# A four-layer kernel: layer 0's chain by quarters, layer 1's norm in two parts, layer 2's end together with layer 3's start

## The chip, the cores and the metric

The kernel runs on one core of one Trainium2 chip. TensorE (PE) multiplies matrices, VectorE (DVE) and ScalarE (ACT) do elementwise work, GpSimd (POOL) does some of it and issues gathers, SyncE (SP) issues most DMAs. Every engine works through its own queue in order, and semaphores let one wait for another. The metric is the device time of one execution in microseconds (us).

## The reference, cut to what matters

The input x has 8 sequences of 512 tokens with 128 channels. Four layers follow, each of the form

```python
xn = _layernorm(x)
x = x + attn(xn) * _silu(ffn(xn))
```

Layer 0's attn is a recurrence over the 512 tokens, for each sequence and each of 16 heads with an 8x8 state S. What follows the recurrence matters here:

```python
sab = einsum('bhvk,bhk->bhv', S, kk_)
S = S * exp(w_)[:, :, None, :] + sab[..., None] * b_[:, :, None, :] + v_[..., None] * k_[:, :, None, :]
y = einsum('bhvk,bhk->bhv', S, r_)
...
yn = (y - y.mean(-1)) / sqrt(var + 0.00064) * ln_w + ln_b
bonus = (r4 * k4 * time_faaaa).sum(-1) * v4
out = (yn + bonus) * g @ output.T
```

Its ffn has 48 experts that each choose tokens. Layer 1 is linear attention with Taylor features and 8 experts that choose 1024 tokens each. Layer 2 is causal attention whose result is refined by 8 iterations `u = tanh(ctx @ w_ctx + xs @ w_x + b)`, `vs += 0.1 * (u - xs - vs)`, `xs += 0.1 * vs`; its ffn is a chain of ternary products. Layer 3 is a Mamba-like mixer, and its ffn is full attention over 512 tokens with 16 heads.

## The kernel before

x lies in SBUF as 32 tiles of 128 tokens (4 per sequence, JT = 4). The program runs layer after layer.

**Layer 0** works in four blocks (jt) of 128 tokens of all sequences; 128 partitions are sequence times head. A block is 64 pair-steps (HT), in 8 chunks of SH = 8. For each pair-step DVE does five pairs of small operations (L747 to L759) on the state, for each chunk also Z (L734, L738) and HR (L761 to L765), the state times r. `outputs` (L691) sums HR over 8 with PE and copies the sum to Y by ACT: `eighths` (L360) is 8 products with the identity, each in two passes, which accumulate in PSUM (L364). Between the chunks `go_on` takes steps of the next block's projections (`front`, L386 to L487, and `back`, L643 to L680: PE turns Kt, Rt, KNt, EWt, Bt, Vt, ACT copies, L663 and its neighbours combine pairs of tokens), and `side` takes steps of the 48 experts. When a block's last chunk is done, the chain L772 to L814 follows for the whole block: own value (L772, L773), mean by eighths (L777), square (L778), variance by eighths, Ln and Exp (L779, L780), bonus (L781), Y times mu (L782), eight scalings by ACT (L784), 32 passes to turn it (L796), gate (L799), and the product with `output` (L804 to L810). For block 3 it ends in x (L813, L814).

In layers 0 to 2 PE's order is the program's (manual_schedule); the other engines' order is made by the framework's scheduler, which moves an instruction ahead where its operands are ready by its own cost model. Pools reserve SBUF; a pool that takes over memory waits for its last users.

**Layer 1** begins with `layernorm`: the 32 tiles in two groups of 16, for each group 16 statistics (L143), seven small operations of 128x16 (L147 to L154), 16 normalisations, 10 of them on DVE (L158) and 6 on ACT (L160). Then 32 transposes (L168) and the first product for k (L1082).

**Layer 2** goes through 128 units of attention; `groups` and `rest` (the output product, the 8 iterations L1557 to L1565, the ternary chain L1580 to L1593 and the sum into x, L1603) are taken in steps beside the units of the next sequence. For the last sequence the steps remain and are run to the end (`layer2`, last two lines).

**Layer 3** then loads its constants and works in an order written out by hand on PE, DVE, ACT and POOL. A unit is one of 128 (sequence, group of heads, key tile): scores (L2089), maxima (L2091), exponentials (L2094), weighing (L2119). `begin` (L1812 on) makes a sequence's features and then its mixer parameters, `mixer` works for one of 32 tiles, `end` finishes a sequence; `fill` takes their steps between the units, with SHARE = 1.75 passes of credit, mixers from unit 9 on every third unit. Steps of `begin` that are still left when a mixer needs them are run in one go. After the units come the last mixers and ends.

Of the kernel before, what the change touches and what calls it, by code (L numbers as in the profile page):

```python
# [20 lines left out]
P = 128  # L21
# [59 lines left out]
class Kern:  # L81
# [53 lines left out]
    def layernorm(self, pool, x, xn, eps, nt=NT, group=16):  # L135

        nc = self.nc
        st = pool.tile([P, nt, 6], F32, name="ln_st")
        var, r, mr = (pool.tile([P, nt], F32, name="ln_" + n) for n in ("var", "r", "mr"))
        for g in range(0, nt, group):  # L140
            sl = slice(g, g + group)
            for j in range(g, g + group):
                nc.vector.bn_stats(st[:, j, :], x[:, j, :])  # L143

            mean = lambda i: st[:, sl, 3 * i + 1]
            dev = lambda i: st[:, sl, 3 * i + 2]
            nc.vector.tensor_tensor(r[:, sl], mean(0), mean(1), ALU.subtract)  # L147
            nc.vector.tensor_tensor(r[:, sl], r[:, sl], r[:, sl], ALU.mult)
            nc.vector.tensor_tensor(var[:, sl], dev(0), dev(1), ALU.add)
            nc.vector.scalar_tensor_tensor(var[:, sl], r[:, sl], C / 4.0, var[:, sl], ALU.mult, ALU.add)  # L150
            nc.vector.tensor_tensor(mr[:, sl], mean(0), mean(1), ALU.add)
            nc.scalar.activation(r[:, sl], var[:, sl], AF.Sqrt, bias=eps, scale=1.0 / C)
            nc.vector.reciprocal(r[:, sl], r[:, sl])
            nc.vector.scalar_tensor_tensor(mr[:, sl], mr[:, sl], -0.5, r[:, sl], ALU.mult, ALU.mult)  # L154
            for j in range(g, g + group):
# [175 lines left out]
def layer0(k, x, A, at):  # L331
# [5 lines left out]
    with ExitStack() as ctx:  # L337
# [212 lines left out]
        w1p_ = pool("l0w", 2)  # L550
        ep = pool("l0e", 2)
# [141 lines left out]
        for jt in range(JT):  # L693
# [79 lines left out]
            nc.vector.tensor_tensor(yp[:, :, 0, :], yp[:, :, 0, :], t3[:, 0:HT], ALU.add)  # L773


            mu = bp.tile([P, P], F32, name="mu")
            nc.vector.scalar_tensor_tensor(Y, Y, 8.0, bc(eighths(Y), 2, 8), ALU.mult, ALU.subtract)  # L777
            nc.scalar.activation(t3, Y, AF.Square)  # L778
            nc.scalar.activation(mu, eighths(t3), AF.Ln, bias=k.eps_gn, scale=1.0 / 8)  # L779
            nc.scalar.activation(mu, mu, AF.Exp, scale=-0.5)  # L780
            nc.vector.tensor_tensor(t3, Vs.rearrange("p t s n -> p (t s) n"), bc(bonus, 2, 8), ALU.mult)  # L781
            nc.vector.tensor_tensor(Y, Y, bc(mu, 2, 8), ALU.mult)  # L782
            for n in range(8):
                nc.scalar.activation(  # L784
                    Y[:, :, n], Y[:, :, n], AF.Identity, scale=cn["ln_w"][:, n : n + 1], bias=cn["ln_b"][:, n : n + 1]
                )

# [4 lines left out]
            for n0 in range(0, 8, 4):  # L792
                ps = k.pa((P, 4, P))
                for i in range(4):
                    for src in (Y, t3):
                        nc.tensor.matmul(  # L796
                            ps[:, i, :], src[:, :, n0 + i], k.ident, start=(src is Y), stop=(src is t3)
# [170 lines left out]
class Layer1:  # L968
# [6 lines left out]
    def __init__(self, k, cp, x, A, at):  # L975
# [3 lines left out]
        self.f_d = k.f1_d  # L979
        self.cn = k.load_consts(cp, A["c1"], at, "c1")  # L980
        self.xT = cp.tile([P, N], F32, name="xT1")
# [332 lines left out]
class Layer2(BySequence):  # L1314


    def __init__(self, k, ctx, x, A, at):
        self.k, self.x = k, x
        nc, tc = k.nc, k.tc
        pool = lambda name, bufs=1: ctx.enter_context(tc.tile_pool(name="l2" + name, bufs=bufs, reuse_waits="tile"))  # L1320
        cp = pool("c")
        self.cn = cn = k.load_consts(cp, A["c2"], at[0], "c2")
        self.fn = fn = k.load_consts(cp, A["f2"], at[1], "f2")

        self.half_s = cp.tile([P, 4], F32, name="half_s")
        nc.vector.tensor_scalar(self.half_s, fn["w1_s"], 0.5, None, ALU.mult)
        self.both_s = cp.tile([P, 4], F32, name="both_s")
# [9 lines left out]
        self.va2 = [cp.tile([P, JT, H * 9 + 23], F32, name=f"va2{i}") for i in range(2)]  # L1337
# [4 lines left out]
        self.mpad = [cp.tile([P, JT, P], F32, name=f"mpad{i}") for i in range(2)]  # L1342
        for t in self.mpad:
            nc.gpsimd.memset(t, 0.0)
        self.sp2 = pool("p", 2)
        self.tp = pool("t", 2)
# [7 lines left out]
    def begin(self, b):  # L1354
# [14 lines left out]
        h = tp.tile([P, JT, C], F32, name="h2", bufs=1)  # L1369
        nc.vector.tensor_tensor(h, xn, bc(r, 2, C), ALU.mult)  # L1370
        yield 0.0
        q["xT"] = tp.tile([P, T], F32, name="xT2", bufs=1)
# [4 lines left out]
        xa = tp.tile([P, T], F32, name="xa2", bufs=1)  # L1377
# [4 lines left out]
        q["qT"] = tp.tile([P, 4, T], F32, name="qT2")  # L1382
        q["kT"] = tp.tile([P, 2, T], F32, name="kT2")
# [224 lines left out]

# [709 lines left out]
```

## Time and profile before

| | us |
|---|---|
| median of three runs | 3602.8 (3601.02 to 3603.73) |
| profiled execution | 3603.68 |
| its span | 3602.0 |
| DVE busy | 2322.8 (64%) |
| PE busy | 2864.4 (80%) |
| ACT busy | 1790.3 (50%) |
| POOL busy | 729.9 (20%) |
| mean granted TensorE clock | 0.862 |
| layer 0's last HR starts | 838.22 |
| layer 1's first k product starts | 891.46 |
| layer 2's last x is added | 2611.36 |
| layer 3's first maxima start | 2626.50 |

Times are from the span's start. The profile's busy time of PE counts matmuls; weight loads (PEld) run beside them. A stretch row gives, for each engine, busy time and number of instructions, then the granted clock (1.00 is full) and the DMA engines' share. A timeline row gives start, duration, engine, line and operation, and in brackets how long the engine had been idle and what ended that. A row of waits gives the total, the number of times and the longest.

### The profile page before, as it was taken

The numbers are of one execution on the slowest core, as the hardware profiler recorded it, in microseconds if no ns is written. First come the engines' busy times: TensorE is split into PE (matmuls) and PEld (weight loads), VectorE is DVE, ScalarE is ACT, GpSimd is POOL, SyncE is SP. The second block draws the span as 40 slices with busy tenths as digits, with TensorE's granted clock in tenths as the row PEclk, the third lists the DMA queues.
The fourth block names the chain that finished last, engine by engine and source line by source line (L and its number), as shares of the span: only waits on it lengthen the run. The fifth ranks groups of instructions, "written<-read, shape, count | busy, mean of one in ns | idle before, by whom it ended". The sixth has DMA issues, their size and how long they took to land.

```text
span 3602.0 us, 46273 instructions
## 1 busy us (share of the span) xinstructions
PE 2864.4 (80%) x16950; PEld 1575.1 (44%) x16950; DVE 2322.8 (64%) x6354; ACT 1790.3 (50%) x3382; POOL 729.9 (20%) x845
## 2 busy tenths in 40 slices
PE   6175868635988898798888898898588798888887
PEld 4154656534444454333334333443235454444443
DVE  7999888896582334435455454554368777777775
ACT  4173646412544455254454554455255565666665
POOL 0012131300225553101111111111112221212221
PEclk8587889766899999899999999999678888888888
DMA  4012121211001222000000000000000000000000
GB/s 121 2 30 44 31 52 32 43 49 34 1 13 37 39 42 47 37 1 1 1 1 1 1 1 1 1 1 1 2 20 1 4 4 3 2 4 4 4 1 7
DMA packets 67523, 64.59 MB, mean 18 GB/s; under 512 B 5344, under 2 KB 59616, under 8 KB 66784
## 3 DMA queue, kind: packets, MB, share of 16 engines
q1 hardware_dynamic: 39264, 42.75, 3.9%
q0 software_dynamic: 19712, 14.69, 3.1%
q10 hardware_dynamic: 8320, 4.19, 0.4%
q8 instruction: 133, 2.18, 0.3%
q14 instruction: 94, 0.77, 0.1%
HBM read 43.80 MB, written 17.83 MB: 17 GB/s over the span
## 4 chain that ended last, share of the span: by engine, by line
PE 34%; DVE 14%; ACT 10%; issue 2%; POOL 1%; DMA 0%; POOLq 0%; ACTq 0%; DVEq 0%; SPq 0%
PE pu L1454 6%; PE ph L1435 5%; PE pu L2089 5%; DVE nm L2091 2%; PE pf L2119 2%; ACT at L2094 2%; PE pf L1503 2%; ACT at L1490 2%; ACT L1490 1%; PE pa L1557 1%; DVE mpad L1469 1%; PE pu L1466 1%; PE pa L1580 1%; PE pa L2132 1%; PE pa L2027 1%
## 5 line engine op out<-in xcount | busy, mean ns | idle before, releaser
L2094 ACT ACTIVATE at<-pu,nm 128x512 f32<-128x512 f32 x512 | 348.0, 691 | 195.9 <-DVE nm L2091 193.4
L2091 DVE TENSOR_REDUCE nm<-pu 128x1 f32<-128x512 f32 x512 | 319.0, 682 | 90.7 <-PE pu L2089 90.6
L2089 PE MATMUL pu<-qT,kT 32*128 32x512 f32 x1024 | 285.8, 732 | 87.6 <-ACT at L2094 87.2
L199 POOL TENSOR_SCALAR_AFFINE_SELECT at<-at 128x512 f32<-128x512 f32 x184 | 125.1, 680 | 1024.4 <-ACT at L1490 878.0
L1469 DVE TENSOR_REDUCE mpad<-pu 128x2 f32<-128x1024 f32 (+3 forms) x256 | 199.0, 819 | 148.8 <-PE pu L1466 148.7
L1128 ACT ACTIVATE at<-pu,rsqrt 128x1024 f32<-128x1024 f32 (+3 forms) x256 | 191.1, 793 | 188.0 <-PE pu L1123 160.7
L1435 PE MATMUL ph<-hid,f 128*128 128x512 f32 x512 | 255.5, 626 | 11.6 <-ACT hid L1436 11.5
L1490 ACT ACTIVATE at<-pu 128x1024 f32<-128x1024 f32 (+3 forms) x256 | 167.0, 701 | 163.7 <-PE pu L1454 162.7
L364 PE MATMUL pa<-HR,ident 128*128 128x128 f32 x512 | 127.8, 418 | 140.2 <-DVE HR L765 140.2
L364 PEld LDWEIGHTS pa<-HR,ident 128*128 128x128 f32 x512 | 112.7, 265 | 150.2 <-DVE HR L765 74.6
L2089 PEld LDWEIGHTS pu<-qT,kT 32*128 32x128 f32 x1024 | 95.3, 212 | 177.9 <-ACT at L2094 162.5
L2119 PE MATMUL pf<-at,va 128*32 128x512 f32 x1024 | 165.0, 723 | 1.9 <-POOL va L2106 1.9
L608 POOL DMA_INDIRECT f_d<-ys,idx x48 | 87.8, 1828 | 384.6 <-ACT ys L607 355.1
L1454 PE MATMUL pu<-kT,qT 32*128 32x512 f32 (+3 forms) x1024 | 134.9, 500 | 30.0 <-ACT at L1490 29.2
L1454 PE MATMUL pu<-qT,kT 32*128 32x512 f32 (+3 forms) x1024 | 128.0, 492 | 20.7 <-DVE mpad L1469 20.2
L1435 PEld LDWEIGHTS ph<-hid,f 128*128 128x128 f32 x512 | 94.1, 198 | 113.2 <-issue 89.2
L2106 POOL TENSOR_TENSOR va<-V,sm 128x32 f32<-128x32 f32 x128 | 33.7, 263 | 489.0 <-DVE sm L2105 488.4
L1123 PE MATMUL pu<-qT,kT 32*128 32x512 f32 (+3 forms) x1024 | 128.4, 507 | 5.3 <-ACT at L1128 4.4
L1066 POOL DMA_INDIRECT f_d<-ys,idx x64 | 102.8, 1606 | 142.7 <-DMA f_d<-ys,idx 86.0
L1490 ACT ACT_TABLE_LOAD x66 | 84.7, 1283 | 87.8 <-PE pu L1454 87.0
L1133 DVE TENSOR_TENSOR at<-at,ceiling 128x512 f32<-128x512 f32 x72 | 49.9, 695 | 105.6 <-ACT at L1128 99.9
L691 ACT COPY Y<-pa 128x128 f32<-128x128 f32 x32 | 8.5, 265 | 208.7 <-PE pa L364 208.7
(621 smaller groups left out, 6772.5 us busy)
## 6 DMA issues: line engine op xcount, KB each, us to landing
w<-in_w_dram SPq DMA_DIRECT2D x24, 512.0 KB
f_d<-zeros ACTq DMA_DIRECT2D x8, 512.0 KB
xn_d<-xn SPq DMA_DIRECT2D x8, 512.0 KB
w<-in_w_dram SPq DMA_DIRECT2D x16, 256.0 KB
w<-in_w_dram SPq DMA_DIRECT2D x24, 128.0 KB
f<-in_f_dram SPq DMA_DIRECT2D x1, 2888.0 KB
xn<-in_x_dram SPq DMA_DIRECT2D x4, 512.0 KB
Gt<-in_x_dram SPq DMA_DIRECT2D x4, 512.0 KB
```

What stands on the lines that cost most here:

```text
L199: self.nc.gpsimd.affine_select(a, a if src is None else src, pattern, ALU.is_ge, 0.0, base=0, channel_multiplier=-1)
L364: nc.tensor.matmul(ps, k.ident, src[:, :, i], start=(i == 0), stop=(i == 7))
L1123: nc.tensor.matmul(pu[:, n, 0:m], q["kT"][r, g // 2, kc * P : kc * P + P], q["qT"][r, g, kc * P :], start=True, stop=True,)
L1128: nc.scalar.activation(at_[:, i : i + 2, 0:m], pu[:, :, 0:m], AF.Square, bias=k.rsqrt2, scale=32.0**-0.5)
L1435: nc.tensor.matmul(ps, fn[n][:, c0 : c0 + P], src[:, i, :], start=(i == 0), stop=(i == 3))
L1454: self.k.nc.tensor.matmul(pu[:, n, 0:m], a[r, c0 : c0 + P], b[r, q0 : q0 + m], start=True, stop=stop)
L1469: nc.vector.tensor_reduce(top[:, i : i + 2, 16 + g % 2], pu[:, :, 0:m], AX.X, ALU.max)
L1490: nc.scalar.activation(at_[:, i : i + 2, 0:m], pu[:, :, 0:m], AF.Exp, scale=8.0**-0.5)
L2089: nc.tensor.matmul(pu, q["kT"][r, kc * P : (kc + 1) * P], q["qT"][r, g, :], start=True, stop=True)
L2091: nc.vector.tensor_reduce(nm[:, n : n + 1], pu, AX.X, ALU.max, negate=True)
L2094: nc.scalar.activation(E[:, n, :], pu, AF.Exp, bias=nm[:, w], accum_out=sm[:, w])
L2119: nc.tensor.matmul(po[i * 32 : i * 32 + 32, :], va[:, kc, c0 : c0 + 32], E[:, i, :], start=(kc == 0), stop=(kc == JT - 1))
```

## The change

First, `layernorm` takes parts. Layer 1's norm is done for the three tiles of each sequence that blocks 0 to 2 have finished (24 tiles) and then for the last ones (8 tiles). Its pools, and those of layer 0's experts, lie at the right end of the memory, apart from layer 0's other pools. In the changed order of DVE 24 statistics, the small operations and six normalisations stand between block 3's chunks, ten normalisations after the last HR; the transposes stay together behind the last tiles.

Second, `settle` does layer 0's chain up to Y times mu for a quarter of a block (two chunks), in three steps that the loop takes one per chunk, in all four blocks; a quarter's sums are products of 32 columns. The fourth quarter and the third's last step follow the last chunk. The bonus is now kept in Vs. L721, L724 and L732 of the changed kernel are the lines L773, L777 and L782 of before; L825 is L799.

Third, layer 2 hands what is left of its last sequence to layer 3 as `k.tail`. Layer 2's pools are split into a left part, which is released before layer 3, and a right part, which is released when the tail is done; layer 3's pools that need that memory are made by `more_pools` then. Layer 3 takes a step of the tail after each step of `begin(0)` and then one or two per unit. `begin` no longer runs on into the parameters, which are a list of their own, the attention's end (`attended`) is split off `end`, and SHARE, EARLY and EVERY change. Layer 2's constants c2 go to the right, too, and are loaded early in layer 1.

```diff
-    def layernorm(self, pool, x, xn, eps, nt=NT, group=16):
+    def layernorm(self, pool, x, xn, eps, parts=None):
         nc = self.nc
-        st = pool.tile([P, nt, 6], F32, name="ln_st")
-        var, r, mr = (pool.tile([P, nt], F32, name="ln_" + n) for n in ("var", "r", "mr"))
-        for g in range(0, nt, group):
-            sl = slice(g, g + group)
-            for j in range(g, g + group):
+        st = pool.tile([P, NT, 6], F32, name="ln_st")
+        var, r, mr = (pool.tile([P, NT], F32, name="ln_" + n) for n in ("var", "r", "mr"))
+        for part in parts or (slice(0, NT // 2), slice(NT // 2, NT)):
+            if parts:
+                tiles = [b * JT + j for b in range(B) for j in range(JT)[part]]
+                pick = lambda a: a.rearrange("p (b j) -> p b j", j=JT)[:, :, part]
+            else:
+                tiles, pick = range(NT)[part], lambda a: a[:, part]
+            for j in tiles:
                 nc.vector.bn_stats(st[:, j, :], x[:, j, :])
+            mean = lambda i: pick(st[:, :, 3 * i + 1])
+            dev = lambda i: pick(st[:, :, 3 * i + 2])
+            pv, pr, pm = pick(var), pick(r), pick(mr)
...
-        w1p_ = pool("l0w", 2)
-        ep = pool("l0e", 2)
+        w1p_ = pool("l0w", 2, side="right")
+        ep = pool("l0e", 2, side="right")
...
+            mu = bp.tile([P, P], F32, name="mu")
+            def settle(c, Y=Y, yp=yp, mu=mu, Vs=Vs, bonus=bonus, kr=kr):
+                pr, tk = slice(c * 16, c * 16 + 16), slice(c * 32, c * 32 + 32)
+                own_v = bp.tile([P, 16, 8], F32, name="own_v")
+                nc.vector.tensor_tensor(own_v, Vs[:, pr, 0, :], bc(kr[:, pr], 2, 8), ALU.mult)
+                nc.vector.tensor_tensor(yp[:, pr, 0, :], yp[:, pr, 0, :], own_v, ALU.add)
+                yield
+                y = Y[:, tk, :]
+                nc.vector.scalar_tensor_tensor(y, y, 8.0, bc(eighths(y), 2, 8), ALU.mult, ALU.subtract)
+                square = bp.tile([P, 32, 8], F32, name="square")
+                nc.scalar.activation(square, y, AF.Square)
+                v = Vs.rearrange("p t s n -> p (t s) n")[:, tk, :]
+                nc.vector.tensor_tensor(v, v, bc(bonus[:, tk], 2, 8), ALU.mult)
+                yield
+                nc.scalar.activation(mu[:, tk], eighths(square), AF.Ln, bias=k.eps_gn, scale=1.0 / 8)
+                nc.scalar.activation(mu[:, tk], mu[:, tk], AF.Exp, scale=-0.5)
+                nc.vector.tensor_tensor(y, y, bc(mu[:, tk], 2, 8), ALU.mult)
+                yield
+            settling = []
             last = None
             for o in range(0, HT, SH):
                 if jt == JT - 1 and o // SH >= HT // SH - JT:
                         nc.vector.tensor_tensor(s_v[:, :, j, :], f, old, ALU.add)
                     else:
                         held = f, old
+                for works in settling:
+                    next(works, None)
                 next(side, None)
                 go_on(3)
                 if last:
                     outputs(*last)
+                    if o // SH % 2 == 0:
+                        settling.append(settle(o // SH // 2 - 1))
+                        next(settling[-1])
...
             outputs(*last)
+            settling.append(settle(3))
             go_on(40)
             ready = made
-            t3 = fp.tile([P, B, C], F32, name="EWt").rearrange("p b (h n) -> p (b h) n", n=8)
-            nc.vector.tensor_tensor(t3[:, 0:HT], Vs[:, :, 0, :], bc(kr, 2, 8), ALU.mult)
-            nc.vector.tensor_tensor(yp[:, :, 0, :], yp[:, :, 0, :], t3[:, 0:HT], ALU.add)
-            mu = bp.tile([P, P], F32, name="mu")
-            nc.vector.scalar_tensor_tensor(Y, Y, 8.0, bc(eighths(Y), 2, 8), ALU.mult, ALU.subtract)
-            nc.scalar.activation(t3, Y, AF.Square)
-            nc.scalar.activation(mu, eighths(t3), AF.Ln, bias=k.eps_gn, scale=1.0 / 8)
-            nc.scalar.activation(mu, mu, AF.Exp, scale=-0.5)
-            nc.vector.tensor_tensor(t3, Vs.rearrange("p t s n -> p (t s) n"), bc(bonus, 2, 8), ALU.mult)
-            nc.vector.tensor_tensor(Y, Y, bc(mu, 2, 8), ALU.mult)
+            for step in chain(*settling):
+                pass
             for n in range(8):
                 nc.scalar.activation(
                     Y[:, :, n], Y[:, :, n], AF.Identity, scale=cn["ln_w"][:, n : n + 1], bias=cn["ln_b"][:, n : n + 1]
                 )
+            added = Vs.rearrange("p t s n -> p (t s) n")
...
-        with tc.tile_pool(name="l1a", bufs=2, reuse_waits="tile") as tp, tc.tile_pool(name="l1a1", bufs=1, reuse_waits="tile") as tp1:
+        right = lambda name, bufs: tc.tile_pool(name=name, bufs=bufs, reuse_waits="tile", side="right")
+        with right("l1a", 1) as tp, right("l1a1", 1) as tp1:
             xn = tp1.tile([P, NT, C], F32, name="xn1")
-            k.layernorm(tp, x, xn, k.eps5)
+            k.layernorm(tp, x, xn, k.eps5, parts=(slice(0, JT - 1), slice(JT - 1, JT)))
...
-        for _ in chain(groups, rest):
-            next(front, None)
+        assert next(front, None) is None
+        k.tail = chain(groups, rest), late.close
...
-        SHARE = 1.75
-        EARLY, EVERY = 9, 3
-        at = lambda b, jt: max(b * U + jt * JT - 2, EARLY + EVERY * (b * JT + jt))
-        mixers, begins, ends = [], [L.begin(0)], []
-        while not L.q or "ready" not in L.q[0]:
-            next(begins[0])
+        SHARE = 1.9
+        EARLY, EVERY = 19, 10 / 3
+        at = lambda b, jt: max(b * U + jt * JT - 2, EARLY + int(EVERY * (b * JT + jt)))
+        mixers, begins, parameters, ends = [], [], [], []
+        tail, release = k.tail
+        for _ in L.begin(0):
+            next(tail, None)
         credit = 0.0
         def fill():
             nonlocal credit
             credit = min(credit, SHARE) + SHARE
-            for works in (mixers, ends, begins):
-                for w in works[:1] if works is begins else list(works):
+            for works in (mixers, begins, parameters, ends):
+                for w in list(works) if works is mixers else works[:1]:
                     if works is mixers or credit > 0.0:
                         cost = next(w, None)
                         if cost is None:
                         else:
                             credit -= cost
+        def whole(works):
+            for w in works:
+                for _ in w:
+                    pass
+            works.clear()
         for n in range(B * U + LAG + 1):
             for b in range(B):
                 for jt in range(JT):
                     if n == at(b, jt):
-                        for w in begins if "cos" not in L.q[b] else ():
-                            for _ in w:
-                                pass
-                            begins.remove(w)
-                            break
+                        if "cos" not in L.q[b]:
+                            whole(parameters)
                         mixers.append(L.mixer(b, jt))
-                if b and n == max((b - 1) * U, at(b - 2, JT - 1) + 4 if b > 1 else 0):
+                if b and n == max((b - 1) * U, 1):
                     begins.append(L.begin(b))
-                if n == max((b + 1) * U + LAG, at(b, JT - 1) + 1):
-                    ends.append(L.end(b))
-                    next(ends[-1])
+                if b and n == b * U - 1:
+                    whole(begins)
+                if b and n == max((b - 1) * U + 8, at(b - 1, JT - 1) + 1 - U, at(b - 2, JT - 1) + 1 if b > 1 else 0):
+                    while "V" not in L.q.get(b, ()):
+                        next(begins[0])
+                    parameters.append(L.parameters(b))
             scores = L.scores(*divmod(n, U)) if n < B * U else iter(())
             next(scores, None)
+            if tail and next(tail, False) is False:
+                tail = None
+                release()
+                L.more_pools()
+                parameters.append(L.parameters(0))
             fill()
             next(scores, None)
             if LAG <= n < B * U + LAG:
-                L.weigh(*divmod(n - LAG, U))
+                b, u = divmod(n - LAG, U)
+                L.weigh(b, u)
+                if u == U - 1:
+                    assert not tail
+                    L.attended(b)
+                    ends.append(L.end(b))
             if 1 <= n <= B * U:
                 L.scale(*divmod(n - 1, U))
+            if tail and n % 2:
+                next(tail, None)
             fill()
         while mixers or ends:
             fill()
```

More of the change, by code (lines that the diff above doesn't have):

```diff
@@ L794, in layer0 @@
                 for i in range(4):
-                    for src in (Y, t3):
+                    for src in (Y, added):
                         nc.tensor.matmul(
-                            ps[:, i, :], src[:, :, n0 + i], k.ident, start=(src is Y), stop=(src is t3)
+                            ps[:, i, :], src[:, :, n0 + i], k.ident, start=(src is Y), stop=(src is added)
                         )
@@ L1335, in __init__ @@
         nc.vector.tensor_scalar(self.g1[:, 1:2], cn["b1"], 100.0, None, ALU.mult)
-        self.va2 = [cp.tile([P, JT, H * 9 + 23], F32, name=f"va2{i}") for i in range(2)]
+        self.va2 = [ap.tile([P, JT, H * 9 + 23], F32, name=f"va2{i}") for i in range(2)]
         for t in self.va2:
@@ L1340, in __init__ @@
             nc.gpsimd.memset(self.by_head(t)[:, :, :, 8:9], 1.0)
-        self.mpad = [cp.tile([P, JT, P], F32, name=f"mpad{i}") for i in range(2)]
+        self.mpad = [ap.tile([P, JT, P], F32, name=f"mpad{i}") for i in range(2)]
         for t in self.mpad:
             nc.gpsimd.memset(t, 0.0)
-        self.sp2 = pool("p", 2)
-        self.tp = pool("t", 2)
+        self.sp2 = right("p", 2)
+        self.tp = right("t", 2)
+        self.bp = pool("b", 2)
         self.ep = pool("e", LAG + 2)
@@ L1607, in layer2 @@
 def layer2(k, x, A, at):
+    late = ExitStack()
     with ExitStack() as ctx:
         ctx.enter_context(k.banks("l2p", pu=2, pf=1, pa=2, ph=1))
-        L = Layer2(k, ctx, x, A, at)
+        L = Layer2(k, ctx, late, x, A, at)
         units = [(b, g, kc) for b in range(B) for g in range(4) for kc in range(JT)]
@@ L1857, in begin, with parameters @@
         q["held"], q["po"] = {}, {}
-        q["ready"] = True
         yield 0.0
-        yield from self.parameters(q)
-    def parameters(self, q):
+    def parameters(self, b):
         k, nc, cn, tp, ap = self.k, self.k.nc, self.cn, self.tp, self.ap
+        q = self.q[b]
         xT = q["xT"]
@@ L2136, in end @@
         nc.scalar.copy(z, ps)
+    def end(self, b):
+        k, nc, fn, tp, q = self.k, self.k.nc, self.fn, self.tp, self.q[b]
+        z = q["z"]
         sq = self.squares(z, JT, "_e")
```

74 lines of the change are left out of this document (41 added, 33 removed).

## The prediction

> **What bounds the kernel now.** I read the page's 40 slices first, then stretches of the span, then the order of events at the two borders that the change touches, and DVE's waits between layer 0's blocks. A slice is 90 us.
>
> ```profile
> span 3602.0 us, 46273 instructions
> DVE  7999888896582334435455454554368777777775
> PEclk8587889766899999899999999999678888888888
> ```
>
> Layer 0's recurrence is slices 3 to 9: DVE is the engine that is nearly full, and the granted TensorE clock is low towards the end of it. Slice 28 is the dip between layers 2 and 3.
>
> ```profile
> core 0: us, PE busy (x) PEld busy (x) DVE busy (x) ACT busy (x) POOL busy (x), PEclk, DMA share, GB/s
> 225.00:838.90 613.90, 398.80 (x2413) 330.18 (x2411) 548.94 (x2780) 282.43 (x579) 132.94 (x94) 0.80 0.18 40
> 838.90:875.30 36.40, 24.72 (x104) 22.61 (x104) 9.49 (x14) 11.19 (x17) 3.74 (x7) 0.68 0.02 2
> 875.30:900.40 25.10, 15.05 (x56) 9.64 (x56) 18.17 (x74) 9.53 (x21) 0.61 (x1) 0.73 0.37 120
> 2544.00:2626.50 82.50, 41.51 (x122) 18.84 (x122) 34.24 (x60) 15.38 (x24) 8.06 (x9) 0.65 0.06 23
> 2626.50:3572.40 945.90, 816.47 (x4390) 432.16 (x4390) 718.27 (x1643) 587.48 (x1551) 202.08 (x314) 0.85 0.01 3
> ```
>
> The rows are: the recurrence (DVE 89% busy; a chunk of 8 steps in which DVE does nothing else takes 14.17 us without a gap, so whatever is put in front of DVE there is paid in full); layer 0's last chain (no engine is full: a chain of waits); layer 1's norm; layer 2's last sequence and layer 3's first head (again a chain: PE 41.5 of 82.5 us); layer 3's 128 units (PE 86%, DVE 76%).
>
> The last chain, from the timeline of all engines (start, duration):
>
> ```profile
> 838.22 0.69 DVE L765 TENSOR_TENSOR HR<-Hs,Rs 128x512 f32<-128x512 f32 x1
> 839.05 4.07 PE L364 MATMUL pa<-HR,ident 128*128 128x128 f32 x16 [10.10 <-DVE HR L765]
> 843.46 0.69 DVE L773 TENSOR_TENSOR Y<-Y,EWt 128x512 f32<-128x512 f32 x1 [4.55 <-ACT Y L691]
> 844.21 4.12 PE L364 MATMUL pa<-Y,ident 128*128 128x128 f32 x16 [1.08 <-DVE Y L773]
> 848.36 1.22 DVE L777 SCALAR_TENSOR_TENSOR Y<-Y,pa 128x1024 f32<-128x1024 f32 x1 [4.21 <-PE pa L364]
> 850.78 4.00 PE L364 MATMUL pa<-EWt,ident 128*128 128x128 f32 x16 [2.46 <-ACT EWt L778]
> 855.21 1.28 ACT L780 ACT_TABLE_LOAD   x1
> 856.84 1.23 DVE L782 TENSOR_TENSOR Y<-Y,mu 128x1024 f32<-128x1024 f32 x1 [0.72 <-ACT mu L780]
> 858.10 4.17 ACT L784 ACTIVATE Y<-Y,c 128x128 f32<-128x128 f32 x8 [1.29 <-DVE Y L782]
> 862.87 1.08 DVE L799 TENSOR_TENSOR Rt<-pa,Gt 128x512 f32<-128x512 f32 x1 [4.81 <-PE pa L796]
> ```
>
> Each sum of eighths is 16 PE passes in 4.0 to 4.1 us. The same chain runs at the end of blocks 0 to 2, but there the next block's recurrence fills most of it; DVE's waits at the second of these ends:
>
> ```profile
> DVE EWt L781 <- PE pa L364: 2.0, 1, 2.0
> DVE Y L777 <- PE pa L364: 2.0, 1, 2.0
> DVE Rt L799 <- PE pa L796: 2.0, 1, 2.0
> ```
>
> With L773's 0.3 that is 6.3 us lost per block end.
>
> **Price of a quarter's sum of eighths.** A quarter still loads the 128x128 identity 16 times and streams 32 columns instead of 128. This form is not in the trace. Nearest rows: L364 itself, 4.0 us; if the columns set the price, 1.0 us. Against the latter stands a row with 8 columns:
>
> ```profile
> L859 PE MATMUL pa<-c,xT x64: 256/256/362, 901.5 to 910.1; 128*128 128x8 f32 x64
> ```
>
> 64 passes in 8.6 us are 0.135 each, and the records start 0.112 apart at full clock; L433's and L585's passes of 128 columns start 0.112 apart too. So the load sets the pace. At the halved clock contiguous 128-column passes (L808) start 0.213 apart. I take 16 x 0.112 = 1.8 us at full clock and 16 x 0.213 = 3.4 at half; at the block ends (granted clock 0.65 to 0.69) 3.4 for the first and 2.4 for the following ones. Ends 1.0 and 4.0 are kept.
> The granted clock was 0.50 in the last chain's first two sums and 0.67 in its third. The Trainium skill, "TensorE: Matmul & The Clock Gate", section "What's actually happening", says that PE runs at half clock until some 3.4 us of sustained activity. By it, sums that follow each other closely would come to 1.8 each from the second on, about 1 us less per block end than I take.
>
> **Part 1: settling by quarters, blocks 0 to 2.** DVE work: five operations per quarter, 2 x 0.25 and 3 x 0.37 (128 and 256 elements, between L773's and smaller rows), 1.6 x 4 = 6.4 us, instead of 0.69 + 0.69 + 1.22 + 1.23 + 1.22 = 5.05: **+1.4** per block.
> New waits inside the loop, from the changed DVE order: the third quarter's L724 comes 2 us of DVE work after L721, whose eighths need 3.4 + 0.2: wait 1.6. The second quarter's L721 follows the back step's L663 directly, but PE has Bt, Vt and then HR's 16 passes (478.1 to 482.0 in block 1) before Y is copied: wait 2, in blocks 1 and 2.
> Block end: on PE, quarter 2's square sum stands between the last HR and quarter 3's Y. From HR's end: HR 4.25, squares to 7.7, Y to 10.1, L724 at 10.2, where DVE is there at 5.6: wait 4.6. Then 0.4, Square 0.65, sum 2.4, Ln 0.37, table 1.28, Exp 0.31: L732 of quarter 3 at 16; DVE is there at 12.4: wait 4. The two L825 (old L799) then come 2.5 and 1.7 us of DVE work later, while L784 and the passes need 4.8 and 3.8: waits 2.3 and 2.1. With 0.3 at L721: 13 instead of 6.3, **+6.7**.
> Blocks 1 and 2: 1.4 + 3.6 + 6.7 = 11.7 each; block 0: 9.7. Sum **+33**; bounds: +7 (sums of 1.0 us, no wait in the loop) and +50 (sums of 4.0).
> The trace has two table loads of 1.28 in each chain, before L779 (Ln) and before L780 (Exp); the first is hidden, the second is in the walk above. The skill's "ScalarE: Activation LUTs", section "Table sets: the hidden batching unit", counts one load for Ln then Exp; the measurement decides. By the page each end would be 1.3 shorter.
>
> **Part 2: block 3 and layer 1's norm.** Into block 3's recurrence, where DVE has no gaps, go 24 statistics x 0.2 = 4.8 (L143: 17 in 3.38), small operations 0.9, six normalisations x 0.26 = 1.6 (ten in 2.63), three quarters x 1.6 = 4.9, and at each L724 a wait: 0.9 to 1.3 us of work behind L721 against 2.0 to 3.6, 2.3 x 3 = 7. Together **+19**. Ten more normalisations fall into the wait for HR: nothing.
> The chain to L732: as above 16.9 instead of 19.2 us from HR, **-2**. After x (875.27): the first k product began at 891.46. Then only 8 tiles remain: 0.8 (statistics of what is last) + 2.4 (small operations) + 0.3 + 32 transposes 7.4 = 11, **-5**. Nothing is saved on the transposes: all 32 stay behind the late tiles on PE. SP now issues expert weights and constants earlier; L585, which uses the weights, was idle for no DMA before: 0. Sum of part 2 **+12**; bounds -5 (no waits, sums of 1.0) and +20.
>
> **Part 3: layers 2 and 3.** From layer 2's last sums (2544.0) to layer 3's first maxima (2626.5) are 82.5 us. Now begin(0) (2610 to 2624.5, 14.5) runs step for step with nine tail steps: output, norm and features (to 2556.2, 12.2) and three of the eight iterations (4.4 each, 13.2), and the first maxima 2 later: 27.4, **-55**. Bounds: 20 (begin's own chain leads) and 42 (both chains added).
> The other five iterations, ternary product and gate, some 40 us of chain, go among units 0 to 7. Priced by form, DVE's work in the units goes from 701 to 717 us; at 945.9/701 = 1.35 us per us that is **+21**. The later start of mixers (unit 19) and the split-off parameters, which take away drained units of 18 to 23 us, spread the same work: -1. So **+20**; bounds 0 (idle DVE and PE take it) and +40 (the chain is paid in full). Layer 3's constants, 5 us of DMA on its chain, are loaded in layer 2's time: in the 55. The closing (3572 to 3602) keeps. Net **-35**.
> c2 is loaded before the combine: **-1**.
>
> **Sum.** 3603.7 (the profiled execution: span 3602.0 and 1.7 around it) + 33 + 12 - 35 - 1 = 3612.7; the median is 0.9 lower than that execution: **3612**.
>
> **Rivals.**
> A, faster: columns, not loads, set the price of a quarter's sum (1.0 us). Then part 1 costs +7 and part 2 nothing: 3603 + 7 - 36 = 3574. For it: L364's strided reads make its passes 0.233 even at full clock. Against it: L859. It decides from about 1.6 us per sum on.
> B, faster: layer 3 takes the tail into its idle time (DVE 24%, PE 14%): part 3 gives -55, 3592. Against it: light units were bound by their own chain.
> C, slower: the tail's 40 us chain sits in front of the units' scores on PE, in order: part 3 gives -15, 3632.
> D: parts cancel within 7 us, e.g. waits in the loop that coincide with the front's own (15 us per block): 3603.
> That the overlap doesn't happen would give 3647; the changed order has the steps interleaved, so it has no share.
>
> **Chances.** A measurement tells 0.2% (7 us) from no change. Forecast (slower, 3610 to 3625) 0.40; C and beyond 0.13; D 0.17; A 0.16; B 0.14. Slower 0.53, same 0.17, faster 0.30. The range leaves out about a tenth on either side: 3576 to 3638. The slower cases' own range is 3610 to 3638.
>
> **What would show it.** PE: 16 passes of a quarter in 1.8 to 3.4 us (A: near 1.0). DVE: waits of some 4 us at L724 and L732 at each block end, 13 in all; blocks 1 and 2, 174 us each (HR to HR), become 186; the last HR ends at 839 + 33 + 19 = 891; from there to the first k product 52.6 us become 46. First layer 3 maxima 27 us after layer 2's last sums; units 966 us. Wrong would be: a block that isn't longer, or units that stay at 946.

## The result, and the profile after

The changed kernel takes 3632.8 us (median of four runs, 3630.34 to 3641.56) against 3603.27 in the same set; the ratio is 1.0083, 95% interval 1.007 to 1.0096. That is 29.5 us slower, where 9 were forecast. The time lies above the forecast's 3610 to 3625, within 1 us of rival C's 3632; whether C's cause is in it, e4 tells. Its profiled execution has a span of 3630.5 us against 3602.0. The page's slices of DVE and of the granted clock:

```profile
span 3630.5 us, 47159 instructions
DVE  7989787877474334634464554554577677777776
PEclk9597888855789999899999999999788888877888
```

The stretches that answer to those of before (recurrence, last chain, norm, border of layers 2 and 3, units of layer 3):

```profile
core 0: us, PE busy (x) PEld busy (x) DVE busy (x) ACT busy (x) POOL busy (x), PEclk, DMA share, GB/s
225.00:891.40 666.40, 444.78 (x2773) 379.76 (x2771) 559.65 (x2879) 327.65 (x648) 125.51 (x90) 0.77 0.17 38
891.40:924.90 33.50, 26.88 (x128) 25.63 (x129) 12.71 (x26) 13.47 (x21) 5.69 (x10) 0.60 0.00 1
924.90:942.20 17.30, 13.01 (x59) 8.45 (x57) 8.34 (x23) 6.63 (x13) 0.61 (x1) 0.87 0.62 195
2584.40:2613.20 28.80, 18.44 (x50) 8.93 (x50) 13.79 (x26) 7.46 (x12) 2.08 (x3) 0.70 0.00 0
2613.20:3603.00 989.80, 867.37 (x4458) 459.69 (x4459) 736.34 (x1672) 601.01 (x1569) 208.04 (x317) 0.83 0.01 3
```

The recurrence is 52.5 us longer, of which DVE is busy only 10.7 more: the rest is waiting. The border shrinks (before, from the same instruction, L1520's reciprocal, it was 81.1 us; now 28.8), and the units are 42 us longer. How far the changed kernel is behind at each point, from the two traces:

| point | before | after | behind | forecast |
|---|---|---|---|---|
| layer 0's last HR ends | 838.9 | 891.4 | +52.5 | +52 |
| x is complete | 875.3 | 924.9 | +49.6 | +50 |
| layer 1's first k product | 891.5 | 933.0 | +41.5 | +45 |
| layer 2's last reciprocal (L1520, now L1556) | 2545.4 | 2584.4 | +39.0 | +44 |
| layer 3's first maxima | 2626.5 | 2613.2 | -13.3 | -11 |
| layer 3's last maxima | 3574.2 | 3603.0 | +28.9 | +9 |

The table names the place of the error before any experiment: at every point up to layer 3's first maxima the sum of what lies before it came out within 5 us, and the units alone are 22 us off.

The last chain, from the timeline:

```profile
891.45 4.08 PE L370 MATMUL pa<-HR,ident 128*128 128x128 f32 x16 [12.09 <-DVE HR L799]
895.35 1.89 PE L370 MATMUL pa<-square,ident 128*128 128x32 f32 x16
895.87 0.29 DVE L721 TENSOR_TENSOR Y<-Y,own_v 128x128 f32<-128x128 f32 x1 [1.90 <-ACT Y L697]
897.07 2.17 PE L370 MATMUL pa<-Y,ident 128*128 128x32 f32 x16
899.27 0.42 DVE L724 SCALAR_TENSOR_TENSOR Y<-Y,pa 128x256 f32<-128x256 f32 x1 [3.12 <-PE pa L370]
900.26 3.62 PE L370 MATMUL pa<-square,ident 128*128 128x32 f32 x16 [1.02 <-ACT square L726]
901.76 1.28 ACT L730 ACT_TABLE_LOAD   x1
904.22 1.28 ACT L731 ACT_TABLE_LOAD   x1
905.78 0.43 DVE L732 TENSOR_TENSOR Y<-Y,mu 128x256 f32<-128x256 f32 x1 [3.57 <-ACT mu L731]
911.12 1.08 DVE L825 TENSOR_TENSOR Rt<-pa,Gt 128x512 f32<-128x512 f32 x1 [4.91 <-PE pa L822]
```

A quarter's 16 passes over 32 columns take 1.89, 2.17 or 3.62 us, never the 1.0 us that the columns would give. DVE's waits at the end of block 1, where 6.3 us were lost before:

```profile
DVE Y L724 <- PE pa L370: 5.3, 1, 5.3
DVE Y L732 <- ACT mu L731: 3.8, 2, 2.7
DVE Rt L825 <- PE pa L822: 3.6, 2, 2.2
DVE Y L721 <- ACT Y L697: 0.3, 1, 0.3
```

They sum to 13.0, as worked out.

### The profile page after: what moved, and what is told of

Read it like the earlier page. It is cut to its first block, busy times and chain, and to the rows that moved or that the text cites. A ratio compares the mean times of both kernels' runs of the same rounds, so it can differ in the third digit from the quotient of the medians.

```text
span 3630.5 us, 47159 instructions
## 1 busy us (share of the span) xinstructions
PE 2932.6 (81%) x17334; PEld 1644.6 (45%) x17334; DVE 2327.0 (64%) x6414; ACT 1841.0 (51%) x3452; POOL 727.9 (20%) x845
## 4 chain that ended last, share of the span: by engine, by line
PE 36%; DVE 13%; ACT 10%; issue 2%; POOL 1%; DMA 0%; POOLq 0%; ACTq 0%; DVEq 0%
PE pu L1490 5%; PE ph L1471 5%; PE pu L2130 5%; PE pf L2160 3%; DVE nm L2132 2%; PE pf L1539 2%; ACT at L2135 2%; ACT at L1526 2%; ACT L1526 1%; DVE mpad L1505 1%; PE pa L1593 1%; PE pa L2173 1%; PE pu L1502 1%; PE pa L2062 1%; PE pa L1624 1%
## 5 line engine op out<-in xcount | busy, mean ns | idle before, releaser
L2130 PE MATMUL pu<-qT,kT 32*128 32x512 f32 x1024 | 293.4, 738 | 78.6 <-ACT at L2135 78.3
```

Of the source, the lines that this page charges most:

```text
L2130: nc.tensor.matmul(pu, q["kT"][r, kc * P : (kc + 1) * P], q["qT"][r, g, :], start=True, stop=True)
```

## The experiments

My theory after the result: layer 0's quarters lose some 41 us through PE round trips that cost a full set of weight loads (e12 leaves about half of that to them); the overlap at the border of layers 2 and 3 gains; and layer 3's units give back more than was forecast, either through the tail's work in them (P) or through the new pace of the mixers (Q). The kernel before had medians of 3595 to 3606 in the several sets of runs, so times are compared by ratio, and stages by the profiled executions.

**e1, the overlap alone.** The kernel before, with all edits from class Layer2 on.

```diff
-        for _ in chain(groups, rest):
-            next(front, None)
+        k.tail = chain(groups, rest), late.close
...
+        for _ in L.begin(0):
+            next(tail, None)
```

> Only layers 2 and 3 changed, layers 0 and 1 as before. Theory (the loss is layer 0's, the overlap is a gain): the changed kernel stands 41 us behind at layer 1's start and 29 at the end, so alone this is about 12 us faster than before: 3591 (3587 to 3596). Rival (the overlap gains only because layer 0 has shifted constants and pools, or loses on its own): 3603 or more.

Measured: 3588.6 us, ratio 0.9948 (0.9934 to 0.9961), span 3588.7. The theory holds: this part is a gain, 17 us against the kernel before in the same set, where 12 were expected.

**e2, the quarters and the norm alone.** The kernel before, with the edits of `layernorm`, the pools' sides and `settle`.

```diff
+            def settle(c, Y=Y, yp=yp, mu=mu, Vs=Vs, bonus=bonus, kr=kr):
...
+            k.layernorm(tp, x, xn, k.eps5, parts=(slice(0, JT - 1), slice(JT - 1, JT)))
```

> Only layers 0 and 1 changed, layers 2 and 3 as before. Theory: the 41 us that the changed kernel is late at layer 1's first product stay to the end: 3644 (3640 to 3648). Rival (part of it is caught up by layer 1 and 2, which waited for constants): 3636 or less.

Measured: 3644.5 us, ratio 1.0113 (1.0098 to 1.0129), span 3638.6. As expected; nothing is caught up later: in the profiles it stands 34.7 us behind at layer 1's first k product and 36.6 at the end. These 34.7 are 7 less than in the changed kernel, though the code up to there is the same: in e2's execution the last HR ends at 884.3, not at 891.4. So one profile tells layer 0's loss to some 7 us only. The ratios of e1 and e2 multiply to 1.006, the changed kernel's is 1.0083; with these intervals it stays open whether the two parts disturb each other.

**e3, the third quarter's last step ahead of the last sum of HR.** The changed kernel with

```diff
+            next(settling[2])
             outputs(*last)
             settling.append(settle(3))
```

> The changed kernel with the third quarter's last step (sum of squares, Ln, Exp, scaling) ahead of the last chunk's sum of HR in each block. Theory (at a block's end DVE waits because PE, in order, does HR's 16 passes, the third quarter's squares and the last quarter's Y one after the other, 16 weight loads each): L724's last wait falls from 5.3 by about 3.4 at the ends of blocks 0 and 1, by less at block 2's (2.4) and 2 in the last chain: about 10 us faster than the changed kernel, 3623 (3617 to 3628). Rival (the wait is for the copy of Y or for ACT's tables, not PE's order): within 3 us of 3633.

Measured: 3634.3 us, ratio 1.006 (1.0037 to 1.0084), span 3632.6. The median is the rival's number, but two of the five runs took 3617.1 and 3618.0, the low end of the theory's range, and the interval holds both answers: the times don't decide. The trace, of a run of 3634.3, says more. The waits at the end of block 1:

```profile
DVE Y L732 <- ACT mu L731: 6.1, 2, 4.3
DVE Rt L826 <- PE pa L823: 3.6, 2, 2.2
DVE Y L724 <- PE pa L370: 1.3, 1, 1.3
DVE Y L721 <- ACT Y L697: 0.3, 1, 0.3
```

The mechanism is there: L724's wait falls from 5.3 to 1.3 here and to 2.9 at the end of block 0. A part of the fall to 1.3 is the clock, since Y's sum took 2.0 us here and 3.6 in the changed kernel. But the price was wrong: the third quarter's L732 now stands ahead of the last HR and waits 1.8 there, the last quarter's waits 4.3 instead of 2.7, and at the end of block 2, where in the changed kernel PE had already been at full clock (sums of 1.9 and 2.3 us), L724 waits 2.9 instead of 2.4. Over the three block ends DVE waits 36 us in both kernels (12.9, 11.3 and 12.2 here, 13.0, 13.0 and 10.2 there). In these two traces moving a PE sum in the queue passed the wait on.

**e4, the tail before the units.** The changed kernel with

```diff
         for _ in L.begin(0):
             next(tail, None)
+        for _ in tail:
+            pass
```

> The changed kernel, but what is left of layer 2 after begin(0) is run to its end before layer 3's units; the pace of layer 3's other work stays. Theory P (the units are 42 us longer because the tail's 27 us of PE passes and 16 us of DVE work come into units that PE already fills to 86%): the border becomes some 40 us longer and the units some 40 shorter: 3633 (3622 to 3645). Rival Q (the tail is nearly free in the light first units; the units lose by the new pace, mixers from unit 19): 3665 to 3675, with units from 48 on at 133 us per sixteen as in the changed kernel.

Measured: 3651.7 us, ratio 1.0133 (1.0113 to 1.0153), span 3646.6, between the two ranges. Neither: from the reciprocal to the first maxima 72.5 us (43.6 more than in the changed kernel), units 966.6 (23 less). So the tail costs 23 us in the units, and the new pace, with the same work as before (DVE is busy 719.5 us in the units, 720.1 before), another 19 (966.6 against 947.7).

**e5, the chain in one piece again.** The changed kernel without `settle`, with the norm in parts and the overlap.

```diff
-            settling.append(settle(3))
...
+            nc.vector.scalar_tensor_tensor(Y, Y, 8.0, bc(eighths(Y), 2, 8), ALU.mult, ALU.subtract)
```

> The changed kernel with the chain in one piece at each block's end as before; the norm in parts and the overlap stay. Theory (the quarters cost all of the loss; the norm in parts puts 24 x 0.2 + 0.9 + 13 x 0.26 = 9 us into block 3's recurrence, where DVE has no gaps, and saves 8 after x): the same as the overlap alone, 3590 (3585 to 3595), and the last HR at 837 + 9 = 846. Rival (statistics hide between the halves of Hs at no cost): HR at 838, 3581.

Measured: 3589.6 us, ratio 0.9966 (0.9953 to 0.9979); span 3579.1, last HR at 841.9. By time it equals e1 within the intervals, as expected (its profiled execution is the fastest of its six and e1's the slowest of its five, so their spans aren't compared); the last HR is 4.7 us later than in e1 (837.2) where 9 were expected. The norm in parts is worth nothing that these runs can tell. The quarters are the whole loss in layer 0.

**e6, quarters in the last block only.**

```diff
-                    if o // SH % 2 == 0:
+                    if jt == JT - 1 and o // SH % 2 == 0:
...
+            if jt < JT - 1:
```

> The changed kernel with quarters in block 3 only, the chain in one piece in blocks 0 to 2. Theory (quarters lose at every block, also in the last: three stops at L724 and L732 and DVE work of some 16 us inside, 3 us won in the chain behind the last HR): 13 us more than with the whole chain, 3603 (3597 to 3608). Rival (in the last block, with nothing behind the chain, quarters pay): 3585 or less.

Measured: 3609.2 us, ratio 1.0009 (0.9998 to 1.002), by the ratios some 15 us more than e5, where 13 were expected; last HR at 860.0, 18 later than in e5, and 1.6 won between it and x. Even in the last block, for which the chain is exposed, quarters lose.

**e7 and e8, mixers from unit 9 again.** Both are e1 with

```diff
-        EARLY, EVERY = 19, 10 / 3
+        EARLY, EVERY = 9, 3
```

and e8 besides with

```diff
-        SHARE = 1.9
+        SHARE = 1.75
```

> The overlap alone (layers 0 and 1 as before), mixers from unit 9 on every third unit as before; SHARE stays 1.9. Theory F (units without a mixer have a floor of 4.4 to 5 us that DVE and ACT don't fill; starting the mixers 10 units later makes ten more of them and crowds 20% more mixers into each later stretch): units 983 become 965 (960 to 972), units from 48 on about 120 per sixteen, the whole 3571 (3565 to 3578). Rival G (the split of begin and parameters, the order of the lists and the pools' waits make the units slow): units stay within 6 of 983, the whole 3583 or more.

> As the run before it, and SHARE back to 1.75. Theory F: as there within 5 us, since a unit's length is set by what its engines do and not by the credit. Rival S (the credit of 1.9 lets steps pile up in front of the scores): 6 us or more faster than with SHARE 1.9.

Measured: e7 (SHARE 1.9) 3606.9 us, ratio 1.0021 (0.9987 to 1.0054); e8 (both lines) 3608.0, ratio 1.0004 (0.999 to 1.0017). Both are slower than e1, against the theory. e8's trace shows both halves of it: from unit 48 on each stretch of 16 units takes 119.5 us, as in the kernel before (in the changed kernel 132 to 135), but one unit, the ninth, takes 53.0: the tail has just ended, sequence 0's parameters can only then begin, and the first mixer, due now, has them run in one go. Units 1001 in all. The rival S is not decided by these two runs, whose times are the same within their intervals. e7's runs fall apart: seven took 3595 to 3609 us, three, the profiled one among them, 3638 to 3645. Its stretches of 126.3 us, which the expectation of e10 compares with e8's 119.5, are thus those of an execution 31 us above the median, and its units are as much longer than e8's (1032 and 1001 us); that SHARE makes the difference isn't shown.

**e9, the quarters' sums on DVE.** The changed kernel with

```diff
-                nc.vector.scalar_tensor_tensor(y, y, 8.0, bc(eighths(y), 2, 8), ALU.mult, ALU.subtract)
+                nc.vector.tensor_reduce(mu[:, tk], y, AX.X, ALU.add)
+                nc.vector.scalar_tensor_tensor(y, y, 8.0, bc(mu[:, tk], 2, 8), ALU.mult, ALU.subtract)
...
-                nc.scalar.activation(mu[:, tk], eighths(square), AF.Ln, bias=k.eps_gn, scale=1.0 / 8)
+                nc.vector.tensor_reduce(mu[:, tk], square, AX.X, ALU.add)
+                nc.scalar.activation(mu[:, tk], mu[:, tk], AF.Ln, bias=k.eps_gn, scale=1.0 / 8)
```

> The changed kernel with both sums of a quarter done by one DVE reduction of 128x256 to 128x32 each (0.4 us by the size of DVE's other rows) instead of 16 PE passes; order, steps and quarters stay. Theory W (what the quarters lose is the PE round trips, 16 weight loads each however few the columns): waits at L724 vanish, those at L732 fall to ACT's part (Ln, one exposed table load, Exp), each block end loses 6 us less, the three stops in block 3 go, the last chain gets 7 us shorter, and DVE has 3 us more work per block: 30 us faster than the changed kernel, 3603 (3592 to 3613). Rival (the quarters lose by ACT's table loads and by the number of instructions): 3622 or more.

Measured: 3582.2 us, ratio 0.9962 (0.9948 to 0.9976), span 3577.1, 53 less than the changed kernel's (by the ratios 43, and 43 up to x by the traces). The reductions take 0.41 us. The waits at the end of block 1:

```profile
DVE Rt L827 <- PE pa L824: 1.9, 2, 1.4
DVE Y L734 <- ACT mu L733: 0.5, 1, 0.5
DVE Y L721 <- ACT Y L697: 0.3, 1, 0.3
```

These are 2.7 us instead of 13.0; the last HR ends at 854.1 instead of 891.4, and from there to x 27.9 us instead of 33.5. The same quarters, steps and Ln and Exp remain, so these 43 us are what the sums cost more on PE than on DVE; they are not the price of the quarters, as e12 shows. The gain is larger than expected because at the block ends the waits at L732 (here L734) go almost entirely as well.

**e10 and e11, two more paces,** on e5: SHARE 1.75 alone (e10), and with mixers from unit 14 on every third besides (e11).

```diff
-        SHARE = 1.9
+        SHARE = 1.75
...
-        EARLY, EVERY = 19, 10 / 3
+        EARLY, EVERY = 14, 3
```

> Chain in one piece, norm in parts, overlap, the new pace of the mixers, but SHARE 1.75. With the old pace 1.9 made each steady stretch of 16 units 6.8 us longer than 1.75 (126.3 and 119.5). Theory (the larger credit lets steps in ahead of the scores): units 984 become 965 (955 to 975), the whole 3570 (3560 to 3580). Rival (with the crowded pace the larger credit is needed, steps left over are run in one go): units 984 or more.

> As the run before it, mixers from unit 14 on every third unit. Theory F (floor of units without mixers, crowded units after): if the parameters of sequence 0 are done by then, units 955 (945 to 965), steady stretches 119.5 from unit 64 on, the whole 3560 (3550 to 3572). Rival (parameters aren't done and are run in one go, as the 53 us unit at mixer start 9): one unit of over 20 us near unit 14 and units 975 or more.

Measured: e10 3578.4 us, ratio 0.9951 (0.9935 to 0.9968), units 986.1, as long as in e5 (983.7): a unit of 37.2 us appears where steps are left over. e11 3603.3 us, ratio 1.0023 (1.0013 to 1.0032), units 1010.6, one of 39.4 at the first mixer: the rivals' answers. 119.5 is reached again, in the stretches from unit 80 to 112.

**e12, one piece, sums on DVE.** e5 with both sums of the chain as reductions, the version that the runs point to.

```diff
+            nc.vector.tensor_reduce(mu, Y, AX.X, ALU.add)
+            nc.vector.scalar_tensor_tensor(Y, Y, 8.0, bc(mu, 2, 8), ALU.mult, ALU.subtract)
...
+            nc.vector.tensor_reduce(mu, t3, AX.X, ALU.add)
+            nc.scalar.activation(mu, mu, AF.Ln, bias=k.eps_gn, scale=1.0 / 8)
```

> Chain in one piece with its two sums as DVE reductions of 128x1024, norm in parts, the overlap with the changed pace: what the runs so far point to. Theory W: two PE sums of 4.1 us become reductions of 1.2 in the last chain (6 us), block ends lose 1 to 2 us less each: 8 to 12 us less than with PE sums in one piece, 3579 as a profiled span becomes 3569 (3564 to 3575), 0.990 of the kernel before. Rival (DVE, which is full in the recurrence, pays 2 x 1.2 us per block and keeps the waits): 3577 or more.

Measured: 3561.0 us, ratio 0.9898 (0.9883 to 0.9913), span 3561.1; last HR at 831.5, x at 862.4 (30.9 later, 37.4 in e5). It is the fastest of all, faster than both kernels. The gain on e5 is 24 us by the ratios, twice what was expected, and the span lies below the range of 3564 to 3575: besides the chain, blocks 1 and 2 are 3.8 and 6.3 us shorter than in e5 (170.3 and 167.6 from last HR to last HR).

e9 and e12 differ in the quarters alone, and neither sums on PE. e9 is slower by 23 us by the ratios, and x is complete 19.6 us later (882.0 and 862.4). With the sums on PE the quarters cost 42 us by the ratios (changed kernel against e5) and 45.6 at x. So about half of what the quarters lose stays when PE does none of their sums, and the rival of e9, ACT's table loads and the number of instructions, isn't out. From the first HR to the last, ACT loads a table 92 times in e9 and 58 in e12, 1.28 us each, and inside blocks 0 to 2 DVE still waits 5.2, 4.5 and 4.5 us at the steps of `settle`. No run separates the loads from the rest of this half.

## Why the prediction was right or wrong

The direction came out, and the time lies 20 us above the sum. It is rival C's time, but not for C's reason: C had the whole 40 us of the tail's chain paid in the units, and e4 shows 23. The other 19 come from the pace of the mixers, which the forecast put at -1 and no rival priced.

**A quarter's sum is priced by its weight loads: right.** Predicted 1.8 at full and 3.4 at half clock; the trace has 1.88 to 1.98 and 3.4 to 3.6. Rival A (1.0) is out.

**Block ends: right.** Predicted 13 us of waits; 13.0, 13.0 and 10.2. The clock was mis-guessed in detail: the ends of blocks 0 and 1 ran at half clock throughout (Y's sum 3.6 instead of 2.4), and at block 2's the clock rose early (1.9 and 2.3). In this stretch at block 1's end (columns as in the stretches above) PE is busy without a gap from 545.0 to 555.8, and still the granted clock is 0.50:

```profile
545.00:560.50 15.50, 14.37 (x64) 14.10 (x64) 7.85 (x41) 5.11 (x8) 0.00 (x0) 0.50 0.01 2
```

The Trainium skill's rule ("TensorE: Matmul & The Clock Gate", "What's actually happening") that some 3.4 us of sustained activity release the clock doesn't fit this row; why the clock stayed low here, no run tells.

**Waits in the loop: near in sum, not in place.** The third quarter's L724 waits 1.35, 1.6 and 0.6 (predicted 1.6). The second quarter's L721 waits 0.75 in blocks 1 and 2, not 2, while the first quarter's L732 waits 4 us in blocks 0 to 2, which I hadn't foreseen. In block 0:

```profile
275.17 3.70 ACT L650 COPY KE<-pa 128x512 f32<-128x512 f32 x4
276.04 1.88 PE L370 MATMUL pa<-square,ident 128*128 128x32 f32 x16
278.89 1.28 ACT L730 ACT_TABLE_LOAD   x1
280.19 0.29 ACT L730 ACTIVATE mu<-pa,eps_gn 128x32 f32<-128x32 f32 x1
280.75 1.28 ACT L731 ACT_TABLE_LOAD   x1
282.05 0.23 ACT L731 ACTIVATE mu<-mu 128x32 f32<-128x32 f32 x1
282.31 0.43 DVE L732 TENSOR_TENSOR Y<-Y,mu 128x256 f32<-128x256 f32 x1 [4.22 <-issue]
```

PE has summed the squares by 277.9, before DVE stops at 278.1. The wait is ACT's, which in its order still copies KE and then loads a table for Ln and another for Exp. All waits at the steps of `settle` in the loop come to 9.1, 7.8 and 7.1 us in blocks 0 to 2, where 1.6, 3.6 and 3.6 were predicted. But DVE's other waits there shrink, most of them for the next block's projections (in blocks 1 and 2 from 13.9 and 14.4 to 8.0 each), which is the cancelling that rival D named. Blocks 0 to 3 became 8.9, 7.4, 8.8 and 27.4 us longer, the first counted from the span's start to its last HR, the others from last HR to last HR; from the prediction's terms follow 6.5, 11.7, 11.7 and 22.2, and blocks 1 and 2 take 183.9 and 182.7 us, not 186. That the last HR is 52.5 us late, with 52 predicted, is so in part luck; in e2, with the same code, it is 45.

**Block 3: its L724 right, the rest too small.** The three L724 wait 2.4, 1.3 and 2.9: 6.6 (predicted 7). Not foreseen were L732, which waits 1.2 and 2.8, and the first L721 with 2.6. The wait for the experts' sums from DRAM (L750, L721 of before) grew from 1.7 to 5.7 us in this execution; in e2's it is 1.2.

**Chain and norm: gain under-sized.** HR to x is 2.9 us shorter (predicted 2): up to the end of L732 it is 4.4 (14.8 instead of 19.2 us), and 1.5 are lost again from there to x, where the granted clock is 0.59 instead of 0.77. The chain above pays a table load for each change between Ln and Exp (901.76, 904.22, each 1.28 us), as worked out, and not one for both as the Trainium skill's "ScalarE: Activation LUTs" ("Table sets: the hidden batching unit") has it. And from x to the first k product the time falls from 16.2 to 8.1 us (8 less, predicted 5). That the finished tiles are normalised in the wait for HR came out as said.

**The border: right.** 52 us less (predicted 55), with three iterations ahead of the first maxima.

**The tail in the units: right in size.** 23 us by e4 against 21 by DVE's work. Rivals B and C, 0 and 40, are out. The base of the 21 was misread: the prediction divides by 701 us of DVE's work, where its own row has 718; by that the rate is 1.32 instead of 1.35 and the term stays 21. That DVE's work sets this price, and not PE's passes, isn't shown.

**The pace: the step that failed.** "The later start of mixers (unit 19) and the split-off parameters ... spread the same work: -1." It costs 19 us (e4 against before). That the splitting doesn't slow the steady stretches is seen in e8, which has the parameters split off and the old pace, and takes 119.5 us for 16 units from unit 48 on, as before. The old rule starts a mixer on every third unit only up to unit 42 and on every fourth from there; the new one starts one every 10/3 units to the end. So 16 units have 4 mixers before and 4.8 after, and 4 of the 32 mixers move behind unit 48. Units 19 to 48, and from 48 on, in the kernel before:

```profile
2747.90:3003.30 255.40, 208.65 (x1129) 118.06 (x1122) 196.22 (x449) 148.18 (x388) 56.97 (x83) 0.83 0.01 3
3003.30:3574.20 570.90, 498.41 (x2750) 263.52 (x2750) 430.13 (x968) 361.44 (x950) 121.92 (x195) 0.86 0.01 3
```

and in e4:

```profile
2764.60:2991.90 227.30, 198.01 (x1039) 108.72 (x1038) 166.38 (x379) 137.73 (x367) 54.01 (x79) 0.82 0.01 2
2991.90:3619.20 627.30, 552.88 (x2960) 301.25 (x2958) 474.21 (x1071) 378.95 (x994) 141.23 (x211) 0.85 0.01 3
```

44 us of DVE's work have moved behind unit 48 (430 to 474) and cost 56, 1.28 us for each. 30 of them came from units 19 to 48, which became 28 us shorter, 0.94 for each. 15 came from the first 19 units (93.7 to 78.9), which became only 9 us shorter (121.4 to 112.0), 0.64 for each: there e4's units 10 to 15, which have no mixer, take 4.1 us each with DVE 68% and PE 97% busy, so it isn't DVE that sets their length. I had priced all work at the mean 1.35 us per us of DVE, by which a move costs nothing. The old start didn't come with the overlap: e8 and e11 show that mixers due before sequence 0's parameters are ready stop everything for 53 and 39 us. Starts between 14 and 19, and another spacing from 19 on, weren't tried, so it is open how much of the 19 us the overlap must pay. That the crowded units are slow because of DVE alone isn't shown: PE is busy 33 us more in e4's units than before for the same layer 3 work, and no run separates the two.

So the 20 us by which the sum was low are: pace 20 (19 instead of -1), tail 2, border 3, less 5 that were won before layer 3.

## What to carry to other kernels

Splitting a chain into pieces pays only if the piece's price falls with its size: price the smallest form by a row that has the fixed part, here a row with 8 columns, and count the round trips between engines, those to ACT too: with no sum left on PE, the quarters still cost half of what they did. Look at where a moved wait goes before moving it; the sums that no longer left DVE (e9, e12) gained what reordering (e3) did not show. When work is moved between stretches, price it at each stretch's own rate: here 0.64 and 0.94 us were won per us of DVE's work where it was taken away, and 1.28 paid where it was put.

## What the runs showed of the hardware

16 fp32 passes with the same 128x128 identity took 1.9 us at granted clock 1.00 and 3.4 to 3.6 at 0.50 for 32 columns, but 3.9 at 1.00 and 4.1 at 0.50 for 128 columns with a stride of 8 elements. In the kernel before, contiguous passes of 128 columns start 0.112 us apart at full clock. That the stride is the reason is likely and wasn't tried by itself. A DVE reduction of 128x256 to 128x32 took 0.41 us: for so small a sum a fifth to a ninth of PE's time. A change of ACT's table took 1.28 us, also between Ln and Exp. Two stretches of 11 us in which PE had no gap (361.1 to 371.8 and 545.0 to 555.8) stayed at clock 0.50.
